# Scan layer of a four-layer network: background items of the first image's early steps, three per turn or spread over twelve turns

## The chip, the cores and the metric

The kernel runs on one core of one Trainium2 chip. The core has five engines with instruction streams of their own: PE (TensorE, matrix multiplies into PSUM), DVE (VectorE), ACT (ScalarE), POOL (GpSimd), and SP (SyncE), which here only issues DMAs. Each engine works through its stream in the order of the program and waits where a semaphore is not yet set. The metric is the device time of one execution in microseconds (us); lower is better.

## The reference, cut to what matters

Four layers work one after the other on images of 64 channels and 64 x 64 pixels, eight of them. Only layer 0 is touched. For each image it does a layer norm over channels, projects to 2 x 128 channels, puts the first half through a 3 x 3 depthwise convolution and a SiLU (this gives `u`), and then runs a selective scan over the 4096 pixels in four directions `k`, with 16 states per channel:

```
dt  = softplus(wst_k . u + dtb_k)          # per direction, 128 channels
B,C = wx_k . u                             # 16 rows each
h_n = exp(dt * A_n) * h_n + (dt * u) * B_n # first-order recurrence over pixels, n = 0..15
y  += sum_n C_n * h_n
```

Then `y` is normalised, multiplied by SiLU of the second half and projected back. Layers 1 to 3 (attention, a small learner with group norm, attention) are as they were.

## The kernel before, in words

`scan_layer` (L203) runs the scan in steps. A step is one direction `k` and one chunk of 1024 pixels; four chunks by four directions make 16 steps per image, 128 in all. The loop over steps is L710; inside it the loop of L726 takes 16 turns, one per state `n`. The order of the work is written out by hand (`manual_schedule`, L696): each engine executes in the order in which the Python code emits.

A turn `n` emits, in this order:

1. `empty` (L619): ACT copies a finished `yps` out of PSUM, if there is one.
2. `bg.before` (L729): one background item is taken from the queue and its first half, `make`, is emitted (PE work).
3. SP loads the broadcast rows `bt` of state n+3 and `ct` of state n+1 (L578), 512 KB each. There are four `bt` and five `ct` buffers, so a load waits until the old content has been used.
4. ACT: `decay` of state n+2, an Exp (L582) into one of three buffers `a`.
5. `unit` (L592): DVE multiplies `bdu = bt * du` (L601; for states 3 and 8 POOL does it two turns earlier, L590), DVE scans `h` (L605), ACT copies the last column as the state (L609), POOL multiplies `ct = ct * h` (L614; that of states 2 and 7 waits for the next turn).
6. `sum_up` (L628): PE adds a `ct` of an earlier turn into `yps` (L642, four instruction records); the first of a step also adds the skip term (L637).
7. `bg.after` (L740): DMAs put off with `bg.later` are issued, then the second half, `use`, of the item before the current one is emitted (ACT, DVE or SP work).
8. L741: extra rounds of `bg.before` and `bg.after`.

After turn 13 of an early step POOL adds the two halves of the next step's softplus (`soft3`, L535) and computes `dus = dt * u` (`step_input`, L555). In turn 15 ACT copies `dus` to PSUM as `du` (`place_input`, L561), on which the next step's first L601 waits.

`early` (L713) is true for image 0 and steps 0, 1 and 2. In these the background makes what the next step needs. The items in `prepare` order are:

- Step 0, 26 items: norm of pixel blocks 3 and 4 (a block is 512 pixels): centre, centre, variance, variance, pause, fetch (SP: variances from DRAM, L312), pause, root (DVE L315 and ACT Sqrt L316), invert (DVE L319; the result goes to DRAM, L320), pause, back (SP, L324), pause, apply, apply (PE L333; DVE L337 and ACT L338), two projections (PE L370, ACT L376 into `pad`); then convolution of blocks 2 and 3 in two items each (PE L408, ten and eight records; the second item's `use` is ACT's SiLU, L417); then six items for the next step: `lower` twice (PE L494, ACT L502, SP store of `bc` L503), `step_size` twice (PE L512, ACT L519), `soft1` (ACT Abs, Exp), `soft2` (ACT Ln, Relu).
- Step 1, 30 items: norm and projection of blocks 5, 6 and 7 (20 items), convolution of blocks 4 and 5 (four), the same six.
- Step 2, 10 items: convolution of blocks 6 and 7 (four), the same six.

All the matmuls of items use two PSUM banks in turn (tag `mm`), so the `make` of an item waits for the `use` of the item two earlier.

The extra rounds are decided by one line:

```
for _ in range(2 * early + late):
```

Of the kernel before, what the change touches and what calls it, by code (L numbers as in the profile page):

```python
# [164 lines left out]
class Background:  # L165
# [23 lines left out]
    def after(self):  # L189
        late, self.late = self.late, []  # L190
        for do in late:
            do()
        if self.last and self.last[0]:
            self.last[0](self.last[1])
        self.last = self.now

    def drain(self):
        while self.queue or self.last or self.late:
            self.before()
            self.after()  # L200


def scan_layer(cm, x_in, w, xh):  # L203

    tc, nc = cm.tc, cm.nc
    with ExitStack() as ctx:
# [59 lines left out]
        bg = Background()  # L266
# [285 lines left out]
        def step_input(ctl):  # L552

            ctl["dus"] = work.tile([DI, CH], F32, name="dus", tag="dus", bufs=1)
            nc.gpsimd.tensor_tensor(ctl["dus"], ctl["dt"], ctl["ut"]["u"], ALU.mult)  # L555

        def place_input(ctl):


            ctl["du"] = psy.tile([DI, CH], F32, name="du", tag="du")  # L560
            nc.scalar.copy(ctl["du"], ctl["dus"])  # L561
# [11 lines left out]
        def load(ctl, n, t):  # L573

            bcr = ctl["bc"].rearrange("(t n) l -> t n l", t=2)
            name = "bt" if t == 0 else "ct"
            ctl[name, n] = bcp.tile([DI, CH], F32, name=name, tag=name, bufs=4 + t)
            nc.sync.dma_start(ctl[name, n], bcr[t, n].unsqueeze(0).broadcast_to([DI, CH]))  # L578

        def decay(ctl, n):  # L580
            ctl["a", n] = work.tile([DI, CH], F32, name="a", tag="a", bufs=3)
            nc.scalar.activation(  # L582
                ctl["a", n], ctl["dt"], AF.Exp, scale=amat[:, ctl["k"], n : n + 1]
            )
# [7 lines left out]
        def unit(ctl, n, nxt):  # L592

            k, state = ctl["k"], ctl["state"]
            a, bt, ct = ctl.pop(("a", n)), ctl.pop(("bt", n)), ctl.pop(("ct", n))
            flip = slice(None, None, -1 if k >= 2 else 1)
            last = 0 if k >= 2 else CH - 1
            z = bt
            if n not in BY_POOL:
                z = psy.tile([DI, CH], F32, name="bdu", tag="bdu")  # L600
                nc.vector.tensor_tensor(z, bt, ctl["du"], ALU.mult)  # L601
            if n == N - 1 and nxt:
                place_input(nxt)
            h = work.tile([DI, CH], F32, name="h", tag="h", bufs=3)
            nc.vector.tensor_tensor_scan(  # L605
                h[:, flip], a[:, flip], z[:, flip],
                0.0 if state is None else state[:, n : n + 1], ALU.mult, ALU.add,
            )
            nc.scalar.copy(ctl["new"][:, n : n + 1], h[:, last : last + 1])  # L609
            ready.append((ctl, n, ct, h))  # L610
            if n + 1 not in BY_POOL:
                while ready:
                    ctl, n, ct, h = ready.pop()
                    nc.gpsimd.tensor_tensor(ct, ct, h, ALU.mult)  # L614
                    pending.append((ctl, n, ct))
# [3 lines left out]
        def empty():  # L619

            if full:
                ctl = full.pop()
                nc.scalar.copy(  # L623
                    ordered(ctl["y"], ctl["k"], ctl["c"]),
                    ctl["ps"].rearrange("p (a b) -> p a b", b=S),
                )
# [33 lines left out]
        def prepare(b, s):  # L660

            if b not in images:
                return None
            u, zd, y = images[b]
            k, c, i = steps(b)[s]
            dt, bc, ut, items, soft3 = project(u, k, c)
            if b == 0 and s < NCH:
                items = later.pop(s, []) + items
            bg.add(items, first=True)
            new = work.tile([DI, N], F32, name="state", tag="state", bufs=3)  # L670
            return dict(
                k=k, c=c, u=u, y=y, dt=dt, bc=bc, ut=ut, soft3=soft3, new=new, state=None,
                first=(i == 0), new_y=(s < NCH),
            )
# [5 lines left out]
        def start(b):  # L680
            u, zd, items, gates, convs = before(b)
            y = io.tile([DI, L], F32, name="y", tag="y")
            images[b] = (u, zd, y)
            bg.add(items[0] + items[1])
            if b == 0:
                bg.add(convs[0] + convs[1])
                for s in range(1, NCH):
                    later[s] = sum(items[s + 1 : s + 2], []) + convs[2 * s] + convs[2 * s + 1]
                later[NCH] = gates
            else:  # L690
                bg.add(gates)
                for conv in convs:
                    bg.add(conv)


        with tc.manual_schedule():  # L696
            start(0)
            bg.drain()
            ctl = prepare(0, 0)
            bg.drain()  # L700
            ctl["soft3"]()
            for n in range(3):
                load(ctl, n, 0)
            load(ctl, 0, 1)
            for n in range(2):
                decay(ctl, n)
            step_input(ctl)
            place_input(ctl)
            for b in range(NB):
                for s in range(4 * NCH):  # L710


                    early, late = b == 0 and s + 1 < NCH, b == NB - 1 and s > 3 * NCH  # L713
                    if s + 1 < 4 * NCH:
                        nxt = prepare(b, s + 1)
                    else:
                        bg.drain()
                        nxt = prepare(b + 1, 0)

                    def ahead(do, m, *args):  # L720
                        if m < N:
                            do(ctl, m, *args)
                        elif nxt:
                            do(nxt, m - N, *args)

                    for n in range(N):  # L726
                        empty()

                        bg.before(n == N - 3)  # L729
                        ahead(load, n + 3, 0)  # L730
                        ahead(load, n + 1, 1)
                        if n < N - 1:
                            ahead(decay, n + 2)
                        ahead(product, n + 2)
                        unit(ctl, n, nxt)
                        if n == N - 1:
                            ahead(decay, n + 2)
                        if len(pending) + len(ready) > LAG:
                            sum_up()
                        bg.after()  # L740
                        for _ in range(2 * early + late):  # L741
                            bg.before()
                            bg.after()

                        if n == (13 if early else 8) and nxt:
                            nxt["soft3"]()
                        if n == (13 if early else 11) and nxt:
                            step_input(nxt)

                        if s == 0 and n == LAG + 2 and b > 0:  # L750
                            bg.add(after(b - 1, images[b - 1][2], images.pop(b - 1)[1]))
                        if late and n == LAG + 2:
                            c = 4 * NCH - s
                            bg.add(after(b, images[b][2], images[b][1], range(2 * c, 2 * c + 2)))
                        if s == (1 if b else NCH) and n == 0 and b + 1 < NB:
                            bg.add(later.pop(NCH, []))
                            start(b + 1)
                    if nxt:
                        if not nxt["first"]:
                            nxt["state"] = ctl["new"]  # L760
                    ctl = nxt
            while pending:
                sum_up()
            empty()
            bg.add(after(NB - 1, images[NB - 1][2], images[NB - 1][1], range(2)))
            bg.drain()

# [1136 lines left out]
```

## Time and profile before

| | |
|---|---|
| median of 3 runs | 12997.07 us (12996.37 to 12998.29) |
| profiled execution | 12995.36 us |
| its span | 12993.6 us |
| start of step 0, first L601 on DVE | 86.46 us |
| start of step 1 | 171.81 us |
| start of step 2 | 262.84 us |
| start of step 3 | 331.72 us |
| start of step 4 | 388.35 us |

The times of steps are counted from the start of the span; they are the starts of the first L601 of each step on DVE in the timeline. In the timeline a line has the start, the duration, the engine, the source line, the operation with its tiles, and in brackets the idle time before it and what ended that. SPq is the sequencer of SP, where a DMA's duration is that of issuing it, not of the transfer. PEld is PE's weight load.

### The profile page before, as it was taken

The page shows a single profiled execution, that of the slowest core. Times are in us where ns is not written, and L with a number is a line of the kernel's source. Part 1 is how long each engine was busy: PE and PEld are TensorE (multiplying, and loading weights), DVE is VectorE, ACT ScalarE, POOL GpSimd, SP SyncE. Part 2 cuts the span into 40 slices and gives each one's busy share as a digit, 9 for nine tenths or more (in the row PEclk, how much of TensorE's full clock was granted, in tenths as well). Part 3 has the DMA queues.
Part 4 walks back from the last instruction along what each step waited for, and adds up shares of the span by engine and source line. Part 5 has one row for each costly group of instructions (what it writes and reads, how often), then busy time and mean ns, then how long its engine had stood idle before and what let it go on. Part 6 is the DMA issues. An engine that isn't in the chain of part 4 may idle for free. (4 is left out here: it accounts for less than half of the span.)

```text
span 12993.6 us, 115955 instructions
## 1 busy us (share of the span) xinstructions
PE 11161.9 (86%) x36395; PEld 4115.1 (32%) x36395; DVE 10881.6 (84%) x7636; ACT 7717.6 (59%) x10047; POOL 6754.4 (52%) x3126
## 2 busy tenths in 40 slices
PE   7788888888888888888887779999996768999999
PEld 2233232232232232232232222323324553333332
DVE  5999999999999999999999958677686786766766
ACT  4676675675675666766765536445465674544544
POOL 4877888878888888788788830000003681000000
PEclk8999999999999999999999989999998888999999
DMA  4888888888889888888888830000001100000000
GB/s 164 301 292 291 308 301 293 306 298 303 300 300 309 296 296 308 300 298 305 297 299 304 295 120 6 24 18 11 17 6 66 39 27 23 6 16 17 6 10 6
DMA packets 686280, 2333.69 MB, mean 180 GB/s; under 512 B 98224, under 2 KB 98896, under 8 KB 683088
## 3 DMA queue, kind: packets, MB, share of 16 engines
q1 hardware_dynamic: 685648, 2326.13, 51.8%
q8 instruction: 290, 4.75, 0.1%
q14 instruction: 342, 2.80, 0.1%
HBM read 2240.69 MB, written 76.28 MB: 178 GB/s over the span
## 5 line engine op out<-in xcount | busy, mean ns | idle before, releaser
L614 POOL TENSOR_TENSOR ct<-ct,h 128x1024 f32<-128x1024 f32 x2048 | 4799.6, 2357 | 1447.1 <-DVE h L605 969.2
L642 PE MATMUL yps<-ct,ident 128*128 128x512 f32 x8192 | 4233.9, 652 | 547.3 <-POOL ct L614 545.3
L605 DVE TENSOR_TENSOR_SCAN h<-a,state,bdu 128x1024 f32<-128x1024 f32 x1344 | 3153.8, 2347 | 227.3 <-ACT state L609 26.7
L915 DVE TENSOR_TENSOR sum<-sum,ex 128x1024 f32<-128x1024 f32 x1920 | 2347.9, 1223 | 770.7 <-ACT ex L908 655.6
L908 ACT ACTIVATE ex<-sc 128x1024 f32<-128x1024 f32 x2048 | 1985.1, 1021 | 1529.8 <-PE sc L903 1529.7
L642 PEld LDWEIGHTS yps<-ct,ident 128*128 128x128 f32 x8192 | 1586.9, 205 | 3164.6 <-issue 1959.1
L582 ACT ACTIVATE a<-dt,amat 128x1024 f32<-128x1024 f32 x2048 | 2333.4, 1142 | 18.1 <-POOL dt L535 14.9
L601 DVE TENSOR_TENSOR bdu<-bt,du 128x1024 f32<-128x1024 f32 x1792 | 2194.9, 1225 | 101.4 <-ACT du L561 46.3
L922 PE MATMUL av<-ex,v 128*64 128x512 f32 x8192 | 1987.8, 606 | 0.0
L609 ACT COPY state<-h 128x1 f32<-128x1 f32 x2048 | 382.9, 187 | 2191.1 <-DVE h L605 2189.4
L903 PE MATMUL sc<-q,k 16*128 16x512 f32 (+1 forms) x8192 | 1656.3, 628 | 5.0 <-ACT ex L908 4.4
L605 DVE TENSOR_TENSOR_SCAN h<-a,bdu 128x1024 f32<-128x1024 f32 x448 | 1024.3, 2286 | 83.5 <-ACT state L609 16.7
L922 PEld LDWEIGHTS av<-ex,v 128*64 128x64 f32 x8192 | 498.2, 136 | 1363.9 <-issue 1360.5
L903 PEld LDWEIGHTS sc<-q,k 16*128 16x128 f32 (+1 forms) x8192 | 562.1, 184 | 1078.8 <-ACT ex L908 743.5
L1220 POOL TENSOR_TENSOR gt<-gt,pad 128x1024 f32<-128x1024 f32 x16 | 34.9, 2180 | 1617.5 <-ACT gt L1219 1538.1
L590 POOL TENSOR_TENSOR bt<-bt,dus 128x1024 f32<-128x1024 f32 x256 | 602.9, 2355 | 8.9 <-DMA bt<-bc 8.8
L408 PE MATMUL vps<-pad,convd 128*128 128x512 f32 x1152 | 534.2, 597 | 5.6 <-ACT z L393 5.6
L605 DVE TENSOR_TENSOR_SCAN h<-a,state,bt 128x1024 f32<-128x1024 f32 x192 | 499.5, 2602 | 15.0 <-POOL bt L590 8.2
L1593 DVE RECIPROCAL r<-e 128x512 f32<-128x512 f32 x128 | 420.7, 3323 | 0.0
L637 PE MATMUL yps<-y,ident 128*128 128x512 f32 x384 | 301.7, 917 | 115.6 <-ACT y L623 115.5
L1596 POOL TENSOR_TENSOR r<-r,half 128x512 f32<-128x512 f32 x128 | 162.7, 1271 | 360.9 <-issue 188.0
L582 ACT ACT_TABLE_LOAD x265 | 340.0, 1283 | 4.7
(402 smaller groups left out, 10325.1 us busy)
## 6 DMA issues: line engine op xcount, KB each, us to landing
bt<-bc SPq DMA_DIRECT2D x2048, 512.0 KB
ct<-bc SPq DMA_DIRECT2D x2048, 512.0 KB
x<-x SPq DMA_DIRECT2D x12, 2048.0 KB
bc<-e SPq DMA_DIRECT2D x256, 64.0 KB
zd<-z SPq DMA_DIRECT2D x64, 256.0 KB
z<-zd SPq DMA_DIRECT2D x64, 256.0 KB
x<-x SPq DMA_DIRECT2D x32, 512.0 KB
part<-x SPq DMA_DIRECT2D x128, 128.0 KB
```

Source lines behind the costliest of these rows:

```text
L408: nc.tensor.matmul(held[0].rearrange("p (r c) -> p r c", c=S), convd[:, t, :], pad[:, j * rows + dy : (j + 1) * rows + dy, dx : dx + S], s ...
L582: nc.scalar.activation(ctl["a", n], ctl["dt"], AF.Exp, scale=amat[:, ctl["k"], n : n + 1])
L590: nc.gpsimd.tensor_tensor(bt, bt, ctl["dus"], ALU.mult)
L601: nc.vector.tensor_tensor(z, bt, ctl["du"], ALU.mult)
L605: nc.vector.tensor_tensor_scan(h[:, flip], a[:, flip], z[:, flip], 0.0 if state is None else state[:, n : n + 1], ALU.mult, ALU.add,)
L614: nc.gpsimd.tensor_tensor(ct, ct, h, ALU.mult)
L642: nc.tensor.matmul(ctl["ps"][:, bass.ts(i, BK)], cm.ident, ct[:, bass.ts(i, BK)], start=False, stop=(n == N - 1),)
L903: nc.tensor.matmul(sc[:, e, :], k[r : r + d, bass.ts(j, 128)], qs[i][r : r + d, :], start=True, stop=True,)
L908: nc.scalar.activation(ex, sc, AF.Exp)
L915: nc.vector.tensor_tensor(sums[i], sums[i], ex, ALU.add)
L922: nc.tensor.matmul(avs[i][r, :], v[:, j, r], ex[:, e, :], start=(j == 0), stop=(j == TQ - 1))
L1593: nc.vector.reciprocal(r[n][s], e[n][:, s])
```

## The change

In the three early steps the two extra rounds per turn are replaced by as many as a new method of `Background` says. With `turns` the number of turns left up to turn 11, it gives the smallest number of extra items for this turn at which the rest of the queue can go out in those turns at the same rate. In other steps nothing changes.

```
+    def surplus(self, turns):
+
+        return max(0, -((turns - len(self.queue)) // (turns + 1)))
...
-                        for _ in range(2 * early + late):
+                        for _ in range(bg.surplus(max(0, 11 - n)) if early else late):
                             bg.before()
                             bg.after()
```

## The prediction

> **What bounds the kernel now.** I read the page first, then busy time in stretches cut at the starts of the steps, then DVE's waits, then the timelines. On the page DVE's busy row is full in the whole scan layer:
>
> ```profile
> span 12993.6 us, 115955 instructions
> DVE  5999999999999999999999958677686786766766
> ```
>
> Stretches of the three early steps and, last, of step 3 (columns: length, then PE, PEld, DVE, ACT, POOL busy, granted clock, DMA share, GB/s):
>
> ```profile
> 86.46:171.81 85.35, 63.92 (x118) 22.92 (x118) 54.92 (x35) 40.75 (x60) 43.05 (x19) 0.82 0.57 196
> 171.81:262.84 91.03, 78.16 (x140) 26.80 (x141) 56.68 (x36) 48.25 (x70) 46.69 (x21) 0.81 0.56 186
> 262.84:331.72 68.88, 52.59 (x110) 20.09 (x108) 54.34 (x30) 36.84 (x51) 46.66 (x21) 0.95 0.70 246
> 331.72:388.35 56.63, 42.32 (x79) 14.77 (x80) 54.33 (x30) 30.30 (x45) 47.72 (x21) 0.91 0.84 293
> ```
>
> Step 3 is what DVE costs: 56.6 us for 54.3 busy. The early steps have the same DVE work plus at most 2.3 us, but last 28.7, 34.4 and 12.3 us longer: 75 us in all, the most that the change can win. DVE's waits from 86.4 to 332 us (waiter, releaser, total, times, longest):
>
> ```profile
> DVE bdu L601 <- ACT du L561: 42.8, 4, 40.1
> DVE h L605 <- ACT state L609: 22.4, 4, 11.8
> DVE h L605 <- ACT a L582: 21.4, 5, 9.5
> DVE xn L337 <- PE rps L333: 14.2, 5, 4.2
> DVE vsm L315 <- DMA vsm<-vard: 13.3, 2, 7.8
> ```
>
> (40.1 of the first is the wait before step 0.) Two kinds: 43.8 us behind ACT in scans, 27.5 us in norm items. The first kind is ACT standing in order behind a SiLU whose convolution is not done, with a decay `a` behind it. In step 0's timeline:
>
> ```profile
> 128.72 1.21 DVE L601 TENSOR_TENSOR bdu<-bt,du 128x1024 f32<-128x1024 f32 x1
> ...
> 138.52 0.69 ACT L417 ACTIVATE u<-vps,convb 128x512 f32<-128x512 f32 x1 [8.76 <-PE vps L408]
> 139.22 1.28 ACT L582 ACT_TABLE_LOAD   x1
> 140.52 1.15 ACT L582 ACTIVATE a<-dt,amat 128x1024 f32<-128x1024 f32 x1
> ...
> 141.75 2.29 DVE L605 TENSOR_TENSOR_SCAN h<-a,bdu 128x1024 f32<-128x1024 f32 x1 [11.83 <-ACT state L609]
> ```
>
> The releaser is named "state", but the `a` that DVE needs ended only just before. SP shows what a small DMA costs behind four loads (step 1):
>
> ```profile
> 193.75 0.67 SPq L320 DMA_DIRECT2D rsd<-vsm  x1
> 201.05 0.25 SPq L324 DMA_DIRECT2D rstd<-rsd  x1
> ```
>
> L324 waits for L320's data: 7.3 us. In step 0, with the queue drained, the same pair lies 1.46 us apart.
>
> **What the Trainium skill says.** "TensorE: Matmul & The Clock Gate", Part 1: PE runs at half clock after about 3.4 us of idleness and warms in a busy window of that length. The trace agrees in kind: one record of L642 takes 0.43 us at 98 us, 0.93 at 110 us after a gap; warming took about 5 us. "ScalarE: Activation LUTs", What ACT_TABLE_LOAD costs: 1283 ns; the trace has the same mean. "DMA: Bandwidth & Descriptors", Queues, rings and completion order: SP has one queue row, whose rings are consumed in order; the pair above agrees.
>
> **The change, part by part.** No work is added or removed; items move to other turns. By the formula, items per turn are: step 0, 3, 3, then 2 in turns 2 to 11 (before: eight turns of 3, then 2); step 1, 3 in turns 0 to 5, then 2 in turns 6 to 11 (before: ten turns of 3); step 2, 1 in turns 0 to 9 (before: 3, 3, 3, 1). So step 1's norm is untouched; only its convolutions and projections move. `soft2`'s use falls in turn 12, one before `soft3`.
>
> *The tail.* Let c be the end of the step's last convolution on PE. After it the new order on ACT is fixed, with durations from the lines above and around: SiLU 0.7; `lower` on PE, first e copy done at c+1.6; table load, decay 12, done c+4; second e copy, first dt, decay 13: c+6.5; PE meanwhile does a sum (1.7) and the last `step_size`, second dt c+8.2; Abs, Exp c+10.4; decay 14 c+11.4; table load, Ln, Relu c+14.8; table load, decay 15 c+17.3, scan 15 c+19.6. On POOL `soft3` (2.35) and `dus` (2.40) end at c+19.6, `du` (1.02) at c+20.7. Both chains end together: the next step starts at c+20.7. Before, it started 33.3 us after c in step 0 (138.5 to 171.8) and 28.0 in step 1 (234.8 to 262.8), because DVE stood at scan 9 or 11, not 12, when c came.
>
> *c in step 0.* Root moves to the end of turn 3, after scan 3, so its wait for data at 102.77 costs DVE 3.2 instead of 5.5 us. `rsd` issues at 103.6, but now behind the loads of turn 4: six loads of 0.52 MB from 96.5 us at the 300 to 350 GB/s seen end near 107, so by the pair above L324 goes at 108.2 and PE has rstd at 109.7 (before 108.2). Apply 1 (cold, 1.9) 111.6; a cold sum 115.3; apply 2 116.5; projection 117.6; sum 119.4; projection 120.4; first conv part 10 x 0.43 = 4.3, 124.7; sum 126.4; 8 x 0.43 = 3.4, 129.9; 4.3, sum 1.7, 3.4: c = 139.3, 0.8 later than before. If PE is warm at 110 us c is 137.5; if it cools again, 141.5. Step 1 starts at 160.0 instead of 171.8: **11.8 us** (9.6 to 13.6). DVE's own sum agrees: waits of 3.2, 0.6 (Sqrt), 1.0, 0.6 (apply), 1.4 (scan 11 behind the first SiLU), 6.7 (scan 12), 2.2 (scan 15), 1.0 (du) = 16.7 instead of 28.8.
>
> *c in step 1.* Norm and its waits stay. The convolution starts on PE at 217.4 as before but with one sum more between its parts: c = 234.8 + 1.7 = 236.5, start of step 2 at 257.2 instead of 262.8 (unshifted): **5.6 us** (3 to 8: at most two sums more or fewer).
>
> *Step 2.* Per turn PE now has half a convolution (3.4 to 4.3) and a sum (1.7; 3.4 with the skip), 5.2 to 7.7 us against DVE's 3.7, for four turns. First SiLU: PE done 6.5 us after the step's start, ACT reaches it at 12.5. Second: PE done at 19.4, ACT there at 18.6, 0.8 us wait; decay 7 then ends at 22.7 and its scan starts at 25.8. So the waits of 7.26, 0.74 and 3.88 us in this step go; I charge 0.4 for `ct` 7, whose buffer is freed late by PE. **11.5 us** (8 to 11.9).
>
> *What it gives elsewhere.* `bc` stores move behind loads of turns 10 and 11, but next step's first `bt` is loaded in turn 13, two turns later; cover 3 us, cost nothing; without it, about 3 us per step. SP's blocked stretch in step 0 (no `bt` or `ct` issued from 121.4 to 142.2) ends, since the store no longer stands ahead of turns 8 to 10's loads. From step 3 on nothing changes and DVE sets the pace (step 3: 96% busy), so the gain goes through to the end.
>
> Sum: 11.8 + 5.6 + 11.5 = 28.9 us. The profiled execution took 12995.36, of which 1.8 lies outside the span; 12995.4 - 28.9 = 12966.5. The median of the runs is 1.7 higher: 12968.2 us, 0.22% less. 0.2%, 26.0 us, is about what a measurement of this kernel can tell from no change.
>
> **Rivals.** *Half the gain* (20%): the norm's DMAs and PE's cold clock set c, not the number of items. If c is 5 us later in steps 0 and 1 the gain is 6.8 + 0.6 + 9, about 16 us: 12981. For it: rsd behind two more loads, 82% granted clock. Against: step 2 has no norm. *More* (11%): c comes earlier since PE stays warm, and step 1's gain doubles: 40 us, 12957. *Slower* (7%): the spread puts sums between the convolution's parts; a sum waits for `ct`, `ct` for its load, the load in SP's queue for an older sum's buffer. If this ring delays c, each us of it is paid in full by the tail. It decides when these delays sum to 28.9 us beyond the ends worked out above; twice that gives 12997.1 + 28.9 = 13026. Against: `ct` is loaded a turn ahead, five buffers deep, and PE's sums trail DVE by two turns at most in step 3. *The change does not act*: half so in step 1, whose first six turns stay at 3; in the sum.
>
> **How the numbers follow.** Likeliest (62%): 12961 to 12975, of which three quarters lie beyond 26 us. Faster: 0.47 + 0.11, some 0.57. Same: 0.15 of the likeliest, 0.20, and 0.02 of the slower one, rounded to 0.38. Slower: 0.05. The bounds of the three terms added give 20.6 to 33.5; to hold 8 in 10 with the half gain and a part of the larger, I take 12958 to 12986.
>
> **What would show it.** Starts of steps 1, 2, 3 near 160, 246 and 303 us; step lengths 73.5, 85.4, 57.4; step 2 without waits on ACT over 1 us; waits of some 7 us at scan 12 in steps 0 and 1; L337's waits in step 1 as before. Wrong if PE's last L408 in step 0 ends after 142 us, if step 1 shows the old 91 us, or if steps after the third grow.

## The result, and the profile after

The changed kernel takes 12967.75 us (median of 11 runs) against 12993.69 us for the kernel before (11 runs): ratio 0.998, 95% interval 0.9972 to 0.9988, that is 16 to 36 us less. The forecast was 12968.2 us. The profiled execution of the changed kernel took 12973.39 us, its span is 12971.5 us.

The same table of stretches as before, for the changed kernel, cut at the starts of its steps 0 to 3 (columns: length, then PE, PEld, DVE, ACT, POOL busy, granted clock, DMA share, GB/s):

```profile
85.86:162.89 77.03, 60.88 (x118) 21.55 (x118) 57.00 (x35) 43.60 (x62) 43.06 (x19) 0.87 0.64 217
162.89:249.88 86.99, 74.26 (x144) 26.48 (x144) 58.40 (x35) 48.25 (x70) 46.67 (x21) 0.88 0.58 198
249.88:307.64 57.76, 47.99 (x106) 18.17 (x104) 54.32 (x31) 37.06 (x52) 46.64 (x21) 1.00 0.83 290
```

The steps are 8.3, 4.0 and 11.1 us shorter, 23.5 us together. Step 3, from one `du` copy to the next, is 55.2 us in both kernels, and the last of the 128 `du` copies comes at 7487.8 instead of 7513.6 us: what the early steps won is still there when the scan layer's last step begins.

DVE's waits from 85.8 to 307.5 us in the changed kernel (waiter, releaser, total, times, longest):

```profile
DVE bdu L605 <- ACT du L565: 46.7, 3, 39.4
DVE h L609 <- ACT state L613: 21.4, 6, 6.8
DVE xn L341 <- PE rps L337: 8.8, 5, 4.9
DVE vsm L319 <- DMA vsm<-vard: 6.9, 2, 3.6
...
DVE h L609 <- ACT a L586: 0.2, 1, 0.2
```

(Lines are four further down than before; 39.4 of the first is the wait ahead of step 0.) Scans behind ACT: 21.6 us where it was 43.8. Norm items: 15.7 where it was 27.5. The waits for `du` at the starts of steps 1 and 2 have grown from 1.8 us together to 7.3, besides the 39.4. (The 2.7 us of the first row before, without the 40.1, hold the start of step 3 too.) DVE's timeline of step 0 shows the waits that are left:

```profile
102.10 2.25 DVE L319 TENSOR_SCALAR vsm<-vsm 128x8 f32<-128x8 f32 x1 [3.26 <-DMA vsm<-vard]
...
134.11 2.29 DVE L609 TENSOR_TENSOR_SCAN h<-a,bdu 128x1024 f32<-128x1024 f32 x1 [1.98 <-ACT state L613]
...
144.42 2.29 DVE L609 TENSOR_TENSOR_SCAN h<-a,bdu 128x1024 f32<-128x1024 f32 x1 [6.75 <-ACT state L613]
...
162.89 1.23 DVE L605 TENSOR_TENSOR bdu<-bt,du 128x1024 f32<-128x1024 f32 x1 [2.95 <-ACT du L565]
```

Root waits 3.26 us for its data (3.2 in the forecast), scan 11 behind the first SiLU 1.98 (1.4), scan 12 behind the second 6.75 (6.7). What is not in the forecast is that L319 takes 2.25 us instead of 0.17, and that `du` is waited for 2.95 us instead of 1.0.

### The profile page after: what moved, and what is told of

Read it like the earlier page. It is cut to its first block, busy times and chain, and to the rows that moved or that the text cites. A ratio compares the mean times of both kernels' runs of the same rounds, so it can differ in the third digit from the quotient of the medians.

```text
span 12971.5 us, 115950 instructions
## 1 busy us (share of the span) xinstructions
PE 11151.7 (86%) x36395; PEld 4110.6 (32%) x36395; DVE 10883.3 (84%) x7636; ACT 7722.4 (60%) x10049; POOL 6752.2 (52%) x3126
## 5 line engine op out<-in xcount | busy, mean ns | idle before, releaser
L586 ACT ACTIVATE a<-dt,amat 128x1024 f32<-128x1024 f32 x2048 | 2333.3, 1142 | 13.9 <-POOL dt L539 10.7
L609 DVE TENSOR_TENSOR_SCAN h<-a,bdu 128x1024 f32<-128x1024 f32 x448 | 1024.6, 2287 | 76.7 <-ACT state L613 15.9
```

Source lines behind the costliest of these rows:

```text
L586: nc.scalar.activation(ctl["a", n], ctl["dt"], AF.Exp, scale=amat[:, ctl["k"], n : n + 1])
L609: nc.vector.tensor_tensor_scan(h[:, flip], a[:, flip], z[:, flip], 0.0 if state is None else state[:, n : n + 1], ALU.mult, ALU.add,)
```

## Experiments

The time of a whole run of one kernel scatters by 10 us and more to either side here, so parts of the change are read from the lengths of the steps in the profile, one profile of each kernel, counted between `du` copies; whole times go with their intervals, each ratio against runs of the kernel before that were taken beside it. The table holds all lengths in us. The tail is the time from the end of the step's last convolution on PE to the next step's first multiply on DVE.

| kernel | step 0 | step 1 | step 2 | tail 0 | tail 1 | median, ratio to before |
|---|---|---|---|---|---|---|
| before | 85.4 | 91.0 | 68.9 | 33.3 | 28.0 | 12993.7 |
| changed | 77.0 | 87.0 | 57.8 | 22.6 | 24.1 | 12967.8, 0.998 (0.9972 to 0.9988) |
| spread in step 0 alone | 79.9 | 89.5 | 68.9 | 22.7 | 28.0 | 12983.3, 0.9993 (0.9985 to 1.0001) |
| spread in step 1 alone | 87.3 | 87.1 | 68.3 | 33.3 | 22.7 | 12989.3, 0.9994 (0.9986 to 1.0003) |
| spread in step 2 alone | 85.4 | 90.8 | 58.1 | 33.3 | 27.9 | 12985.1, 0.9992 (0.9984 to 1.0001) |
| before, four taps left out | 79.4 | 82.7 | 62.0 | 34.7 | 28.0 | 12962.0, one run |
| changed, four taps left out | 72.9 | 80.7 | 57.8 | 24.4 | 26.0 | 12949.6, one run |
| before, bc stores by ACT | 88.5 | 90.5 | 68.9 | 35.5 | 28.3 | 12997.0, 1.0 (0.9992 to 1.0009) |
| changed, bc stores by ACT | 78.5 | 85.3 | 57.7 | 21.1 | 21.1 | 12965.9, 0.9979 (0.9972 to 0.9987) |
| changed, root's add by ACT | 77.5 | 85.4 | 57.6 | 23.0 | 22.7 | 12962.3, one run |
| changed, rsd and rstd by ACT | 81.3 | 86.7 | 58.2 | 22.5 | 22.2 | 12961.3, one run |
| all three by ACT | 76.5 | 88.5 | 58.6 | 21.0 | 21.3 | 12971.0, 0.9982 (0.9976 to 0.9989) |
| thirteen turns | 75.5 | 81.6 | 57.3 | 20.8 | 20.8 | 12955.9, 0.9972 (0.996 to 0.9984) |
| thirteen turns, bc stores by ACT | 82.2 | 81.8 | 57.4 | 20.7 | 20.9 | 12960.9, 0.9971 (0.9961 to 0.9981) |

### Each step alone

```
-for _ in range(bg.surplus(max(0, 11 - n)) if early else late):
+for _ in range(bg.surplus(max(0, 11 - n)) if early and s == 0 else 2 * early + late):
```

and the same with `s == 1` and `s == 2`.

> The spread in step 0 alone; steps 1 and 2 keep three items per turn. Theory (each step loses time to its own convolutions and its own in-order queues): step 0 as in the changed kernel, 77 us; steps 1 and 2 as before, 91 and 69 us; 8 us off the kernel before. Rival (the steps are coupled: a shorter step 0 hands its backlog to step 1): step 1 grows by 2 us or more and the total gain is under 6 us.

> The spread in step 1 alone. Theory: step 0 85.4, step 1 87, step 2 69 us; 4 us off the kernel before. Rival (coupled): step 1 within 1 us of the old 91, its gain coming only from a shorter step 0 ahead of it.

> The spread in step 2 alone, one item per turn. Theory: steps 0 and 1 as before, 85.4 and 91; step 2 57.8 us; 11 us off the kernel before, the largest of the three. Rival (coupled): step 2 stays over 60 us, since it starts with step 1's old backlog.

The step with the spread becomes short, the others keep their old lengths, within the 2 us by which step 0 scatters here without the spread (85.4 to 87.3; with it 77.0 and 79.9, for the reason shown under PE's pace below). Only step 1 after a spread step 0 is 1.5 us shorter, where the rival had it grow by 2. There the variances are fetched (L316) 15.4 us into step 1, as in the changed kernel, instead of 19.6, and the convolutions start 44.1 us into it instead of 45.6; with step 1 alone spread the fetch stays at 19.7. Off the median of the kernel before in that comparison (12994.9 us) the three are 11.6, 5.6 and 9.8 us, 27.0 together, about what the whole change brings; each interval alone still touches 1.0. So by the lengths of the steps the three are separate causes that add; what a spread step 0 hands on to step 1 is a gain of 1.5 us and no backlog.

### A shorter convolution

```
 return [
-    (part(0, 5), None), (part(5, 9), use)]
+    (part(0, 5), None), (None, use)]
```

with the last matmul's stop moved to the fifth tap of the first image.

> The kernel before, with four of the nine taps (eight of 18 matmul records a block, 3.4 us) left out of the first image's convolutions. Theory (ACT stands behind the SiLU whose convolution PE has not done): each early step does two convolutions, so each is some 6.9 us shorter: 78.5, 84 and 62 us. Rival (SP's queue and the loads set the steps): under 3 us off each.

> The changed kernel with the same four taps left out. Theory: steps 0 and 1 still end a fixed time after the last convolution on PE, and are 6 to 7 us shorter: 70 and 80 us; step 2 hides its convolutions behind DVE and stays at 57.8 us within 0.7. Rival (loads set the steps): steps 0 and 1 under 3 us shorter.

Two half convolutions are 6.9 us of PE. Before, they are worth 6.0, 8.4 and 6.9 us in the three steps; in the changed kernel 4.1, 6.3 and 0.0. In steps 0 and 1 the convolution on PE is on the path in both kernels; in step 2 the spread took it off altogether. Step 0 of the changed kernel missed its forecast of 6 to 7 us. From first to last record its convolutions are 8.6 us shorter, since a sum between their parts goes as well, but they started 38.0 us into the step, 2.7 later than in the changed kernel, for the reason shown under PE's pace below. And the tails are not fixed, as the theory had them: they are 24.4 and 26.0 us instead of 22.6 and 24.1, since PE now does a sum between the last convolution and `lower`, and ACT's first e copy waits 2.0 us for it in both steps instead of 0.3.

### SP's queue

```
-bg.later(lambda: nc.sync.dma_start(
+bg.later(lambda: (nc.scalar if own else nc.sync).dma_start(
     bc[:, bass.ts(i, BK)], e[: 2 * N, bass.ts(i, BK)]
```

where `own` is true for what the early steps make.

> The kernel before, with the bc stores of steps 0 to 2 issued by ACT in place of SP, so that loads of bt and ct no longer stand behind them. Theory (decays behind the SiLU on ACT cost the time, SP's blocked stretch is mostly cover): 0 to 4 us off in all. Rival (SP's blocked stretch is what the change removed): 12 us or more off, half of the change's gain without any spreading.

> The changed kernel with the bc stores of steps 0 to 2 issued by ACT. Theory (the 1.9 and 3.4 us by which the tails of steps 0 and 1 overran their sum come from ct loads behind the second bc store on SP, by way of POOL): steps 0 and 1 go to about 75 and 84 us, step 2 stays; 5 us off the changed kernel. Rival (the tail overran for ACT's own order): under 1 us off each.

In the kernel before nothing is won: 88.5, 90.5 and 68.9 us, ratio 1.0. SP's longest stretch without a load did shrink, from 21.4, 19.6 and 16.9 us in the three steps to 12.3, 10.6 and 7.8 (in the changed kernel it is 8.7, 10.6 and 4.4), so it was cover and not a cause. The edit brought a wait of its own, for ACT's Abs overwrites `e` and waits for the stores to be done, 2.0 us in step 0; but with it taken off step 0 is no shorter than before either. In the changed kernel the tails go from 22.6 and 24.1 to 21.1 us, close to the 20.7 of the sum. The mechanism is in step 1's timelines of SP, POOL and ACT; first the changed kernel, where the last convolution ends at 225.8:

```profile
227.40 3.34 SPq L507 DMA_DIRECT2D bc<-e  x2
...
231.67 0.34 SPq L582 DMA_DIRECT2D ct<-bc  x1
```

```profile
237.00 2.35 POOL L618 TENSOR_TENSOR ct<-ct,h 128x1024 f32<-128x1024 f32 x1 [8.48 <-DMA ct<-bc]
241.68 2.34 POOL L618 TENSOR_TENSOR ct<-ct,h 128x1024 f32<-128x1024 f32 x1 [2.33 <-DMA ct<-bc]
243.98 2.34 POOL L539 TENSOR_TENSOR dt<-dt,e 128x1024 f32<-128x1024 f32 x1
```

```profile
239.58 1.04 ACT L536 ACTIVATE dt<-dt 128x1024 f32<-128x1024 f32 x1
```

The second store waits for ACT's second e copy, and the `ct` of states 12 and 13 stand behind it. POOL multiplies `ct` 13 until 244.0 and only then gets to softplus, whose inputs ACT had ready at 240.6. With the stores on ACT's queue, where the last convolution ends at 228.6:

```profile
235.69 2.35 POOL L618 TENSOR_TENSOR ct<-ct,h 128x1024 f32<-128x1024 f32 x1 [3.93 <-DMA ct<-bc]
240.28 2.35 POOL L618 TENSOR_TENSOR ct<-ct,h 128x1024 f32<-128x1024 f32 x1 [2.23 <-DMA ct<-bc]
243.75 2.35 POOL L539 TENSOR_TENSOR dt<-dt,e 128x1024 f32<-128x1024 f32 x1 [1.13 <-ACT dt L536]
```

The two multiplies start 7.1 and 11.7 us after the convolution instead of 11.2 and 15.9, and softplus waits for ACT, as in the forecast. Of the 5 us expected only the tails' 1.5 and 3.0 appear: the sum of the three steps is 221.6 us, as in the changed kernel (221.8), since in this profile the convolutions ended 3.0 us (step 0) and 1.4 us (step 1) later in their steps. The tails of the other kernels with twelve turns, all taps and the stores on SP lie between 22.2 and 23.0 us, so the stores cost 1 to 3 us of a step.

### Why L319 took 2.25 us

```
-nc.vector.tensor_scalar(sm["v"], sm["v"], 1e-5, None, ALU.add)
-nc.scalar.activation(sm["v"], sm["v"], AF.Sqrt)
+nc.scalar.activation(sm["v"], sm["v"], AF.Sqrt, bias=epst)
```

> The changed kernel with the root's add of 1e-5 done by ACT as the bias of its Sqrt in place of DVE's L319 (in the norms of all images). Theory (L319's 2.25 and 1.89 us in steps 0 and 1, where 0.17 is its cost, are a wait for a port that POOL's multiply holds): DVE's first multiply of turn 4 in step 0 starts 17.0 to 17.3 us after the step's first L605, in place of 18.9; step 0 is 1 to 2 us shorter at an equal pace of PE. Rival (the 2.25 us come from the data's arrival): no change, 18.9 us.

(In this kernel and the next, lines are one further down than in the changed kernel.) In the changed kernel root's data comes while POOL multiplies (a multiply from 101.98 to 104.33 us), and L319 ends at 104.35. The Trainium skill, "SBUF — State Buffer", Who interferes with whom, says that VectorE's `tensor_scalar` can enter a mode that takes the port pair shared with GpSimd, and that whichever of the two comes second is blocked until the first is done. The numbers agree. Twelve kernels here, the one before among them, leave the add on DVE, which makes 24 of these instructions in steps 0 and 1. Fifteen met a multiply of POOL at work and took 1.83 to 2.33 us, each ending within 0.05 us of the end of that multiply; the nine that met none took 0.17. With the add on ACT the timeline of DVE is, in a step that started at 87.24:

```profile
103.79 0.20 DVE L324 RECIPROCAL vsm<-vsm 128x8 f32<-128x8 f32 x1 [3.58 <-ACT vsm L321]
103.91 1.21 DVE L606 TENSOR_TENSOR bdu<-bt,du 128x1024 f32<-128x1024 f32 x1
```

DVE goes on 16.7 us after the step's start instead of 18.9, the theory's number and a little better, though the data came at the same point: ACT's Sqrt starts 16.2 us into the step here, L319 did in the changed kernel. That rules out the rival. The reciprocal takes its 0.20 us beside a multiply of POOL and is not held up. But step 0 is no shorter (77.5), so this part of the forecast was missed: rstd's issue stays where it was, 22.8 us into the step instead of 22.9, though rsd was issued 2.2 us earlier in it. It comes some 2 us after the loads ahead of rsd are through in both kernels, so these seem to set it, and DVE waits for PE's rps later instead.

### Small DMAs on another queue

```
-nc.sync.dma_start(sm["r"], rs.rearrange("(j f) -> j f", j=nb))
+own.dma_start(sm["r"], rs.rearrange("(j f) -> j f", j=nb))
```

and the same for rsd, with `own` ACT's queue.

> The changed kernel with the norm's rsd store and rstd load of the first image's norms issued by ACT in place of SP, on another queue row. Theory (rsd stands behind the loads of bt and ct in SP's row, 4.0 and 5.7 us between the two issues): the two issues lie 1.5 to 2.5 us apart in steps 0 and 1, PE's first rps starts 2 us earlier after rsd in step 0 and 3 in step 1; the steps are 1 to 3 us shorter. Rival (the transfers share the same 16 engines, so another row does not help): 4 and 5.7 us as before.

This theory fell. ACT's sequencer shows the pairs of step 0 and step 1:

```profile
109.44 0.35 ACTq L325 DMA_DIRECT2D rsd<-vsm  x1
112.98 0.25 ACTq L329 DMA_DIRECT2D rstd<-rsd  x1
190.72 0.33 ACTq L325 DMA_DIRECT2D rsd<-vsm  x1
195.89 0.26 ACTq L329 DMA_DIRECT2D rstd<-rsd  x1
```

They lie 3.5 and 5.2 us apart, against 4.0 and 5.7 on SP, and 4.4 and 6.2 in the kernel with all three edits below. On SP this gap scatters from 2.2 to 6.1 us in the step 0 of other kernels with the spread, and from 5.4 to 7.3 in step 1 of all kernels. So a queue row of its own did not get the small transfer past the 512 KB loads here. And rsd is issued 3.8 us after the reciprocal has started, in place of 0.2, for on ACT it stands in order behind a state copy; then rstd's load waits on ACT for rsd to land, and the decay behind it stands still for 3.65 and 5.29 us. Whether the cause of the gap is the shared engines or the load on the memory was not told apart.

### All three together

> The changed kernel with three edits: bc stores and the norm's rsd and rstd on ACT's queue, the root's add in ACT's Sqrt. Theory: tails of 21 us after the last convolution, norm waits shorter by 2 us in step 0 and 4 in step 1: steps of 74, 82 and 57.7 us, 6 to 9 us off the changed kernel. Rival (ACT is the in-order engine of the tail, and DMAs issued there cost what they save): within 2 us of the changed kernel.

No better than the changed kernel, so the rival's side, though a little outside its 2 us: 12971.0 us and three steps of 223.5 us together, against 12967.8 and 221.8. The tails are 21.0 and 21.3, but rsd is issued 1.1 us (step 0) and 2.1 us (step 1) later in the steps than in the changed kernel. The two moves that shorten a wait do not pay where another wait takes its place.

### Thirteen turns

```
-bg.surplus(max(0, 11 - n))
+bg.surplus(max(0, 12 - n))
```

> The changed kernel with the items spread over thirteen turns (0 to 12) in place of twelve; softplus still follows in turn 13. Theory (the last convolution is set by PE and the norm, the tail by ACT's order after it): step 2 the same; steps 0 and 1 within 3 us of the changed kernel, later convolutions against a DVE one turn further on. Rival (an even spread is what pays, so wider is better): both 3 us or more shorter.

> Thirteen turns, and the bc stores of steps 0 to 2 issued by ACT. Theory (with thirteen turns POOL has one multiply, not two, between the bc stores and softplus, so that the stores no longer delay the tail, which is 20.7 us in both steps): tails stay at 20.7 to 21.0 us and the time is that of thirteen turns alone, within 4 us. Rival (the stores in SP's queue still cost the tail or the convolution some time): 3 us or more off steps 0 and 1 together.

Step 0 is 1.5 us shorter and step 1 is 5.4, which fits neither: the theory allowed 3 us, and the rival wanted 3 or more in both. Two causes can be read off. The tails are 20.8 us in both steps, for with every item a turn later only one `ct` multiply, not two, stands on POOL between the stores and softplus; with the stores moved to ACT as well the tails stay at 20.7 and 20.9, as expected. And in step 1 the third apply no longer follows in the turn of the second. DVE's waits in step 1 of the thirteen-turn kernel:

```profile
DVE h L609 <- ACT state L613: 7.5, 2, 6.7
DVE vsm L319 <- DMA vsm<-vard: 4.2, 1, 4.2
DVE xn L341 <- PE rps L337: 2.8, 3, 2.0
```

L341's waits are 2.8 us, against 7.8 in step 1 of the changed kernel. Of step 1's 5.4 us the shorter tail makes 3.3, and 2.1 come from convolutions that end earlier in the step; that the third apply's turn is what moved them was not tested alone. By the three steps (214.5 us against 221.8) this version is ahead of both kernels, and its median, 12955.9 us, is the lowest of the full kernels; its interval against the kernel before overlaps that of the change, so that in whole times it is shown to beat the kernel before, and not to beat the change. With the stores by ACT it took 12960.9 us, 5.0 more and so outside the forecast's 4, though the ratios to the kernel before are alike (0.9971 and 0.9972). Its step 0 is 82.2 us, and the tail has no part in that.

### PE's pace

From PE's first rps of step 0 to its first convolution lie the same sixteen matmul records in all kernels whose step 0 is spread over twelve turns. PE in the changed kernel:

```profile
110.42 1.93 PE L337 MATMUL rps<-rstd,ident 2*64 2x512 f32 x2 [4.06 <-DMA rstd<-rsd]
...
115.99 1.19 PE L337 MATMUL rps<-rstd,ident 2*64 2x512 f32 x2
117.11 1.12 PE L374 MATMUL xps<-xn,win 64*128 64x512 f32 x2
118.16 1.98 PE L646 MATMUL yps<-ct,ident 128*128 128x512 f32 x4
...
121.13 4.56 PE L412 MATMUL vps<-pad,convd 128*128 128x512 f32 x10
```

and in the kernel with the spread in step 0 alone:

```profile
109.24 1.93 PE L337 MATMUL rps<-rstd,ident 2*64 2x512 f32 x2 [1.61 <-ACT state L613]
...
114.81 1.97 PE L337 MATMUL rps<-rstd,ident 2*64 2x512 f32 x2
116.70 2.07 PE L374 MATMUL xps<-xn,win 64*128 64x512 f32 x2
118.71 3.78 PE L646 MATMUL yps<-ct,ident 128*128 128x512 f32 x4
...
123.83 4.56 PE L412 MATMUL vps<-pad,convd 128*128 128x512 f32 x10
```

From the second apply on, the records take 1.7 to 1.9 times as long in the second. From the first rps to the convolution it is 10.7 us in one and 14.6 in the other (14.3 with the bc stores by ACT). The program of this step is the same in the two kernels; what differs is when PE's clock came back. In stretches of 2 us the granted clock is 0.50 from 110 us in both; it is back at 1.00 from about 116.3 us in the first and 123.2 in the second, with PE busy all the while from the first rps on. This is why the same step 0 takes 77.0 us in one profile and 79.9 in another. With thirteen turns and the stores by ACT the clock stays at 0.50 until about 129.7 us. From rps to the convolution it is then 15.2 us, against 10.3 with thirteen turns alone, and the convolutions take 1.5 us more: 6.4 of the 6.7 us by which that step 0 is longer. So the busy window of about 3.4 us that the prediction cites for warming is not what these profiles show: 5.9, 13.9 and 18.3 us of unbroken work passed at half clock. What makes the clock come back early or late was not found.

## Why the prediction was right, point by point

- **The bound.** Right. DVE's waits in the three early steps were the time to be won, and all that was won there reached the end: 23.5 us of shorter steps (and 0.6 us of an earlier start) in a profile whose span is 22.1 us shorter; 25.9 us between the medians. That the median came within 0.5 us of the forecast is luck: the gain was 3.0 us smaller than the 28.9 forecast, and the kernel before ran 3.4 us faster in the eleven runs of the comparison than in the three from which the forecast counted.
- **The tail.** Its mechanism, ACT's fixed order after the last convolution, was right, and so was 20.7 us, wherever POOL is free: 21.1 with the stores moved, 20.8 with thirteen turns. In the changed kernel it measured 22.6 and 24.1. The term that was mis-sized is the cost of the bc stores, put at nothing because "next step's first `bt` is loaded in turn 13, two turns later". That looked at `bt` alone, but the loads that pay are `ct` 12 and 13, by way of POOL: 1.5 and 3.0 us. The price named for the case without cover, about 3 us per step, was near.
- **c in step 0.** Forecast 52.8 us into the step, measured 54.4, and in further profiles with the same norm 54.4 (root's add by ACT), 57.1 (step 0 alone) and 57.4 (bc stores by ACT). Of the 1.6 us, 1.3 is a later rps (24.6 us into the step instead of 23.2). The loads ahead of rsd were through near 106.5 us, 20.6 us into the step and so when they were forecast to be, but rstd's issue followed 2.3 us later where 1.2 was allowed. PE's pace was left as a range of 4 us, and the runs show one as wide, but placed later: the likeliest value, 10.7 us from the first rps to the convolution, is near the fast end of the runs' 10.2 to 14.6. So the sign named for being wrong, a last L408 after 142 us, did not show in the changed kernel (140.3) but did in the last two of these (143.0 and 143.2). L319's wait for POOL's port was not foreseen and, going by the run with the add on ACT, cost nothing.
- **The steps.** Step 0: 8.3 us for 11.8, below the term's 9.6; c was 1.6 us late and the tail 1.9 long. Step 1: 4.0 for 5.6. Its convolutions ended 62.9 us into the step, 1.8 earlier than worked out, since the norm did not stay as it was: the fetch of variances came 4.2 us earlier in the step, and root waited 3.6 us for them instead of 7.8. The longer tail took that back, so two errors met here. Step 2: 11.1 for 11.5, its ACT waits gone as worked out, with one wait of 0.5 us left.
- **The small DMAs.** The 7.3 us of rsd and rstd in step 1 were put down to the order in SP's queue row. On a row of their own the pair took 3.5 to 6.2 us, where it takes 2.2 to 7.3 on SP in the kernels with the spread, so that order is not shown to be the cause.
- **The rivals.** Half the gain: its mechanism, the norm's DMAs and PE's cold clock, took 1.6 us of c in step 0 in the changed kernel, but 4.3 and 4.6 in two other profiles, near the 5 that the rival wanted; in step 1 c was early. More: step 1's gain did not double. Slower: a sum waiting for `ct` was not what held the convolutions, which took 19.2 us from start to end, sums between them included, against 18.9 worked out; the stores did reach POOL, but for 4.5 us in all. That step 1's first six turns kept three items each is seen in L341's wait of 4.9 us, and in what a thirteenth turn was worth.

## What to carry to other kernels

Count a background chain from its slowest producer: what matters is not how evenly items are spread but how far the foreground has got when the producer is done, and what each in-order engine must still do after it. A DMA that waits in a queue costs the data behind it, so name every load queued behind a moved store and who reads each one. Where an engine's clock falls in waits, one profile of a stretch of 80 us can be off by 3 us and more (77.0 and 79.9 for the same program); compare its parts, and several profiles.

## What was not expected of the hardware

A `tensor_scalar` of 128 x 8 or 128 x 12 on DVE took 1.8 to 2.3 us while POOL ran a multiply, and 0.17 us without. Among loads of 512 KB, a 4 KB store issued by ACT and the load that depends on it lay 3.5 us apart, and a pair of 6 KB 5.2, hardly less than on SP with the same loads; 1.46 us was the gap on SP with the queue drained. The same sixteen records of PE took 10.2 to 14.6 us by when the clock came back, and in one profile it stayed at half for 18 us of unbroken work on PE.
